# Pair sums of the gate and up products: diagonal results copied by ScalarE, banks opened with differences

## The chip, the cores and the metric

One Trainium2 chip, one of its cores. The metric is device time in microseconds. All data are float32. The engines are named as the profile names them: PE (TensorE, matmul), PEld (its weight loads), DVE (VectorE), ACT (ScalarE), POOL (GpSimd) and SP (SyncE, which issues most DMAs).

## The reference: what is computed

A residual layer of gated experts on x of shape (8, 512, 256), with 8 experts and one shared expert of width F = 1024:

```
g = einsum('bsd,edf->ebsf', h, Wg);  u = einsum('bsd,edf->ebsf', h, Wu)
expert_outs = einsum('ebsf,efd->ebsd', silu(g) * u, Wd)
expert_output = einsum('be,ebsd->bsd', gating_probs, expert_outs)
shared = einsum('bsf,fd->bsd', silu(h @ Sg) * (h @ Su), Sd)
x = x + (1 - sg) * expert_output + sg * shared
```

The kernel treats the shared expert as a ninth one. What follows is about g and u: for every expert, block of 128 columns of F and batch, a 128x512 result with a contraction over 256.

## The kernel before, in words

The work is cut into 36 *units*: 2 halves of four batches, 9 experts, 2 groups of four 128-column blocks (lines 249 to 261). A unit needs, for m = 0 (gate) and m = 1 (up), all 16 products c_ij of weight block i and batch j. A product has two halves of the contraction and would be two matmuls. The kernel saves matmuls: with numbers CI = (0, 1, -1, 2) given to the four blocks, it shifts batch i's first half by CI (line 163) and block i's second half by CI (`make_at`, line 286), so that a *diagonal* product is exact:

- `P_step` (line 370): P_i is the first matmul of c_ii. ACT copies it out of PSUM to SBUF (line 377).
- `Q_step` (line 402): the second matmul lands on the same bank (line 404), which then holds c_ii = P_i + Q_i. DVE takes Q_i = c_ii - P_i out of it (line 410).
- The two off-diagonal products of a pair (i, j), six pairs in `PAIRS`, cost three matmuls in place of four. `R1_step` (line 424) multiplies the difference of weights U by the difference of batches V (line 432), called UV below. Then c_ij = (P_i + Q_j) - UV + W_0 B_0 and c_ji = (P_j + Q_i) + UV + W_1 B_1; `R_step` (line 439) does the last matmul of each (line 445).

The sums z_ij = P_i + Q_j, and where they are made, are what the change is about. For most pairs POOL makes them from SBUF copies (line 389); for `ZBANK` = 2 pairs one of the two sums is made by DVE from the bank that still holds P (line 391). DVE then writes z_ij - UV into a fresh bank (line 436) and adds z_ji onto the bank of UV (line 437). For two *late* pairs (`LATE`, or `LATE0` in the first unit) no z is made: P alone goes in at lines 436 and 437, and DVE adds Q after the last matmul (line 450). In the first unit pair 0 is `PLAIN`: four matmuls for two products, for each m (line 417), and no forms of x before them; its forms are made later for the other units (`make_forms`, line 171).

`finish` (line 355) ends a product: for m = 0 ACT takes silu of the bank (line 358), for m = 1 DVE multiplies silu, gate weight and bank (line 364) into h. `down` (line 467) multiplies h with the down weights with two PSUM banks of its own, `po`, which ACT opens with the running sum (line 482) and copies back (line 506).

Order: PE and POOL keep the order of the program text, ACT does so in the first unit, and a scheduler places DVE, the rest of ACT and SP when the kernel is built. PE's order is written in strings (lines 621 to 624): G is one step of gate and up, D one matmul of the down product of the unit before. Within a unit the G steps are: Q0, P1, P2, Q1, Q2, P3, R1 of pair 0, Q3 (two each, m = 0 and 1), then for each pair p and each m: R1 of pair p + 1, and two R of pair p. The first unit has no D. Gate and up have three PSUM banks for each m (`ps_g`), so a new bank waits for a `finish`.

Of the kernel before, what the change touches and what calls it, by code (L numbers as in the profile page):

```python
# [9 lines left out]
F32 = mybir.dt.float32  # L10
AF = mybir.ActivationFunctionType
ALU = mybir.AluOpType
# [4 lines left out]
def kernel(  # L17
# [31 lines left out]
    nc = tc.nc  # L49
    B, S, D = x.shape  # L50
    E, _, F = Wg.shape
    P = 128
# [4 lines left out]
    NH = B // NI  # L57
    CI = (0.0, 1.0, -1.0, 2.0)
    PAIRS = ((1, 0), (0, 2), (3, 0), (1, 2), (3, 1), (3, 2))
    ZBANK = 2  # L60
    LATE = (4, 5)
    LATE0 = (3, 5)

    PLAIN = (0,)

    const = ctx.enter_context(tc.tile_pool(name="const", bufs=1))
    wpool = ctx.enter_context(tc.tile_pool(name="w", bufs=5))
# [5 lines left out]
    ppool = ctx.enter_context(tc.tile_pool(name="p", bufs=16))  # L73
# [4 lines left out]
    zpool = ctx.enter_context(tc.tile_pool(name="z", bufs=6))  # L78
# [7 lines left out]
    ps_o = ctx.enter_context(tc.tile_pool(name="ps_o", bufs=1, space=PSUM))  # L86
# [4 lines left out]
    gp = nc.gpsimd  # L91
    ve = nc.vector
# [31 lines left out]
    turned = [False, False]  # L124
# [60 lines left out]
    def store_made():  # L185
        for h, p, tiles in made:
            scratch[h, p] = dram.tile([P, 3, S], F32, tag=f"xs{h}_{p}", name=f"xs{h}_{p}")
            for k, t in enumerate(tiles):
                nc.sync.dma_start(scratch[h, p][:, k], t)
        made.clear()  # L190
# [59 lines left out]
    for h in range(NH):  # L250
        for e in range(NE):
            for g in range(GRP):
                u = Unit()
                u.n, u.h, u.e, u.g = len(units), h, e, g
                u.opens = e == 0 and g == 0
                u.closes = e == NE - 1 and g == GRP - 1
                u.name = f"{h}_{e}_{g}"
                u.raw, u.at, u.U, u.W, u.V, u.VB = {}, {}, {}, {}, {}, {}
                u.Ps, u.Qs, u.z, u.bank, u.h_ = {}, {}, {}, {}, {}
                u.wd, u.T, u.sg, u.store = {}, {}, {}, []  # L260
                units.append(u)

# [23 lines left out]
    def make_at(u, i):  # L286
# [9 lines left out]
            return  # L296
        scaled_sum(t, CI[i], raw[:, :, 0], raw[:, :, 1], False)
        u.at[i] = t

    def late(u):  # L300
        return LATE if u.n else LATE0

    def plain(u, p):
        return u.n == 0 and p in PLAIN

# [43 lines left out]
                1: a11, 2: a12, 3: s[:, 3], 4: a22, 5: s[:, 0], 6: s[:, 1], 7: s[:, 2]  # L349
            }  # L350

    def new_bank(u, m, name):
        return ps_g.tile([P, S], F32, tag=f"g{m}", name=f"{name}{m}_{u.name}")

    def finish(u, m, i, j, bank):
        if m == 0:
            s = spool.tile([P, S], F32, tag="sg", name=f"sg{i}{j}_{u.name}")
            nc.scalar.activation(s, bank, AF.Silu)  # L358
            u.sg[i, j] = s
        else:  # L360
            b = NI * u.h + j
            pool, tag = (hapool, "ha") if j < 2 else (hbpool, "hb")
            t = pool.tile([P, S], F32, tag=tag, name=f"h{i}{j}_{u.name}")
            ve.scalar_tensor_tensor(  # L364
                t, u.sg[i, j], coef[:, u.e, b : b + 1], bank, ALU.mult, ALU.mult
            )
            u.h_[i, j] = t


    def P_step(u, i, m):  # L370
        bank = new_bank(u, m, f"c{i}{i}")
        u.bank[i, i, m] = bank
        nc.tensor.matmul(  # L373
            bank, u.raw[i][:, m, 0], xhub[u.h, i][:, 0], start=True, stop=True
        )
        t = ppool.tile([P, S], F32, tag="p", name=f"P{i}{m}_{u.name}")
        nc.scalar.copy(t, bank)  # L377
        u.Ps[i, m] = t
        for p in range(ZBANK):
            a, b = PAIRS[p]  # L380
            if max(a, b) == i and not plain(u, p):
                new_z(u, p, m, i, bank if u.n or p else None)

    def new_z(u, p, m, i, bank=None):

        o = sum(PAIRS[p]) - i
        z = zpool.tile([P, S], F32, tag="z", name=f"z{i}{o}{m}_{u.name}")
        if bank is None:
            gp.tensor_tensor(z, u.Ps[i, m], u.Qs[o, m], ALU.add)  # L389
        else:  # L390
            ve.tensor_add(z, bank, u.Qs[o, m])  # L391
        u.z[i, o, m] = z

    def make_z(u, p, m):
        if p in late(u) or plain(u, p):
            return
        for i in PAIRS[p]:
            o = sum(PAIRS[p]) - i
            if (i, o, m) not in u.z:
                new_z(u, p, m, i)  # L400

    def Q_step(u, i, m):
        bank = u.bank[i, i, m]
        nc.tensor.matmul(  # L404
            bank, u.at[i][:, m], xhub[u.h, i][:, 1],
            start=False, stop=True, skip_group_check=True,
        )
        finish(u, m, i, i, bank)
        t = ppool.tile([P, S], F32, tag="p", name=f"Q{i}{m}_{u.name}")
        ve.tensor_sub(t, bank, u.Ps[i, m])  # L410
        u.Qs[i, m] = t

    def plain_step(u, p, m, r, k):
        i, j = PAIRS[p] if r == 0 else PAIRS[p][::-1]
# [6 lines left out]
        if k:  # L421
            finish(u, m, i, j, u.bank[i, j, m])

    def R1_step(u, p, m):
        i, j = PAIRS[p]
        if plain(u, p):
            for k in range(2):
                plain_step(u, p, m, 0, k)
            return
        bank = new_bank(u, m, f"c{j}{i}")  # L430
        u.bank[j, i, m] = bank
        nc.tensor.matmul(bank, u.U[p][:, m], u.V[p], start=True, stop=True)  # L432
        seed = new_bank(u, m, f"c{i}{j}")
        u.bank[i, j, m] = seed
        first = u.Ps if p in late(u) else u.z
        ve.tensor_sub(seed, first[(i, m) if p in late(u) else (i, j, m)], bank)  # L436
        ve.tensor_add(bank, bank, first[(j, m) if p in late(u) else (j, i, m)])  # L437

    def R_step(u, p, m, r):
        if plain(u, p):  # L440
            plain_step(u, p, m, 1, r)
            return
        i, j = PAIRS[p] if r == 0 else PAIRS[p][::-1]
        bank = u.bank[i, j, m]
        nc.tensor.matmul(  # L445
            bank, u.W[p][:, r, m], u.VB[p][:, r],
            start=False, stop=True, skip_group_check=True,
        )
        if p in late(u):
            ve.tensor_add(bank, bank, u.Qs[j, m])  # L450
        finish(u, m, i, j, bank)


# [98 lines left out]
    def gate_up(u, nxt):  # L552

        def differences(p):
            x_difference(u, p)
            w_difference(u, p)

        def sums(p):
            x_sums(u, p)
            w_sums(u, p)  # L560

        for p, make in ((0, w_difference), (0, w_sums), (1, w_difference), (1, w_sums)):
            make(u, p)
        if u.n:
            make_at(u, 3)
        w_difference(u, 2)
        ahead = ((0, x_difference), (0, x_sums), (1, x_difference), (1, x_sums), (2, x_difference))
        if u.n:
            for p, make in ahead:
                make(u, p)  # L570
        for kind, i in (
            ("Q", 0), ("P", 1), ("P", 2), ("Q", 1), ("Q", 2), ("P", 3), ("R", 0), ("Q", 3),
        ):
            for m in range(2):
                if kind == "Q":
                    Q_step(u, i, m)
                    if i == 1:
                        make_z(u, 0, m)
                    if i == 3:
                        make_z(u, 1, m)  # L580
                elif kind == "P":
                    P_step(u, i, m)
                    if u.n == 0 and m == 1 and i in (1, 3):
                        for p, make in ahead[:2] if i == 1 else ahead[2:]:
                            make(u, p)
                else:
                    R1_step(u, 0, m)
                yield
        for p in range(len(PAIRS)):
            last = p + 1 == len(PAIRS)  # L590
            if p + 3 < len(PAIRS):
                differences(p + 3)
            if nxt is not None:
                if p >= 2:
                    load_w(nxt, p - 2)
                    if p < 5:
                        make_at(nxt, p - 2)
            store_forms(u)
            if u.n == 0 and p == 4:
                for q in PLAIN:  # L600
                    make_forms(0, q)
            if p == 5:
                store_made()
            for m in range(2):
                if not last:
                    R1_step(u, p + 1, m)
                elif nxt is not None:
                    P_step(nxt, 0, m)
                yield
                if p + 2 < len(PAIRS):  # L610
                    make_z(u, p + 2, m)
                for r in range(2):
                    R_step(u, p, m, r)
                    if p == 5 and m == 0 and r == 1:
                        T_sums(u, 0, 5)
                        load_d(u, (0,))
                    if m == 1 and r == 1 and p + 2 < len(PAIRS):
                        sums(p + 2)
                    yield
# [129 lines left out]
```

## Time and profile before

| what | value |
|---|---|
| time, median of 3 runs | 2517.44 us (2516.77 to 2517.63) |
| the profiled execution's own time | 2517.02 us |
| its span in the trace | 2514.9 us |
| busy in the span: PE | 2498.6 us, 99% |
| POOL | 1922.3 us, 76% |
| DVE | 1492.6 us, 59% |
| ACT | 1143.4 us, 45% |
| PE's busy time from 0 to 80 us, in steps of 20 | 17.86, 19.30, 15.98, 20.00 us |
| DVE's busy time in the same steps | 8.54, 15.55, 19.15, 17.09 us |
| DMA | mean 97 GB/s |

A 128x512 float32 matmul is two records in the trace, so 5900 PE records are some 2,950 matmuls and transposes. Busy time is the length of all records of an engine without overlap; the mean duration that a group shows (592 ns for a 128x512 matmul) is that of one record, and records overlap. From one matmul to the next in a full stream it is 0.858 us. Idle time of an engine that is not the bound costs nothing by itself; what counts is PE's idle time, 16 us of the span, and whether new work ends before PE needs it.

### The profile page before, as it was taken

Reading aid. Unit: us, or ns where it says so; the run is one execution under the profiler, and the core shown is the slowest. Engines: PE = TensorE matmul, PEld = TensorE weight load, DVE = VectorE, ACT = ScalarE, POOL = GpSimd, SP = SyncE. Lnnn points to the kernel's source line nnn. Section 1 sums busy time; section 2 is a strip of 40 time slices with the busy share of each in tenths; the row PEclk is TensorE's granted clock in tenths of the full one; section 3 lists DMA queues with packets and bytes.
Section 4 is the critical chain, followed back from the end, with each engine's and each line's share of the span. In section 5 each row is a group of like instructions: output and inputs, shape, how many; then the busy total and the mean of one; then the engine's idle time right before and its main releaser. Section 6 shows DMA issues by size and latency. Waiting matters only on the chain.

```text
span 2514.9 us, 22103 instructions
## 1 busy us (share of the span) xinstructions
PE 2498.6 (99%) x5900; PEld 1108.3 (44%) x5900; DVE 1492.6 (59%) x2242; ACT 1143.4 (45%) x2078; POOL 1922.3 (76%) x2080
## 2 busy tenths in 40 slices
PE   8999999999999999999999999999999999999999
PEld 3444444444444444444444444444444444444444
DVE  7655555565555555565785555555555555555556
ACT  3344444444444444444333444444444444444443
POOL 6877877777777778877798777877777777777874
PEclk9999999999999999999999999999999999999999
DMA  4332232233333323233444322323233332332222
GB/s 159 116 90 84 88 95 89 84 101 96 100 92 93 92 88 88 85 93 94 151 135 119 98 88 84 92 88 89 88 95 100 97 96 88 100 88 81 89 85 80
DMA packets 181180, 242.94 MB, mean 97 GB/s; under 512 B 13888, under 2 KB 122432, under 8 KB 181056
## 3 DMA queue, kind: packets, MB, share of 16 engines
q1 hardware_dynamic: 180768, 241.49, 32.0%
q8 instruction: 49, 0.80, 0.1%
q14 instruction: 75, 0.61, 0.1%
q10 hardware_dynamic: 288, 0.04, 0.0%
HBM read 227.84 MB, written 13.63 MB: 96 GB/s over the span
## 4 chain that ended last, share of the span: by engine, by line
PE 97%; DVE 1%; issue 0%; DMA 0%; POOL 0%; ACT 0%; SPq 0%; DVEq 0%; ACTq 0%
PE po L491 34%; PE c L445 29%; PE c L432 14%; PE c L373 10%; PE c L404 10%; DMA xin<-in_x_dram 0%; PE pto L136 0%; PE ptx L136 0%; POOL z L389 0%; DVE h L364 0%; DVE v L200 0%; PE c L417 0%; DVE c L436 0%; DVE c L437 0%; DVE b L216 0%
## 5 line engine op out<-in xcount | busy, mean ns | idle before, releaser
L445 PE MATMUL c<-b,wb 128*128 128x512 f32 x1720 | 810.6, 592 | 1.0 <-DVE c L436 0.5
L389 POOL TENSOR_TENSOR z<-P,Q 128x512 f32<-128x512 f32 x430 | 538.4, 1281 | 111.0 <-DVE Q L410 69.0
L364 DVE SCALAR_TENSOR_TENSOR h<-sg,coef,c 128x512 f32<-128x512 f32 x576 | 427.1, 742 | 231.6 <-PE c L445 221.6
L506 ACT COPY acc<-po 128x512 f32<-128x512 f32 x477 | 279.0, 585 | 589.0 <-PE po L491 586.1
L358 ACT ACTIVATE sg<-c 128x512 f32<-128x512 f32 x576 | 342.4, 595 | 382.2 <-PE c L445 196.0
L445 PEld LDWEIGHTS c<-b,wb 128*128 128x128 f32 x1720 | 325.9, 190 | 409.6 <-issue 387.3
L464 POOL TENSOR_TENSOR T<-h,h 128x512 f32<-128x512 f32 x284 | 358.3, 1278 | 137.1 <-PE po L491 92.8
L491 PE MATMUL po<-T,sd 128*128 128x512 f32 x864 | 435.3, 593 | 2.0 <-ACT to L543 1.6
L432 PE MATMUL c<-v,u 128*128 128x512 f32 x860 | 433.7, 592 | 3.0 <-DVE h L364 2.0
L436 DVE TENSOR_TENSOR c<-z,c 128x512 f32<-128x512 f32 x286 | 198.6, 694 | 330.2 <-ACT sg L358 255.7
L464 POOL TENSOR_TENSOR T<-h,T 128x512 f32<-128x512 f32 x284 | 356.5, 1278 | 6.8 <-PE po L491 6.8
L450 DVE TENSOR_TENSOR c<-c,Q 128x512 f32<-128x512 f32 x288 | 200.4, 697 | 187.2 <-PE c L445 186.9
L284 POOL TENSOR_TENSOR wb<-wb,u 128x256 f32<-128x256 f32 x216 | 154.5, 738 | 204.6 <-ACT wb L283 204.6
L491 PE MATMUL po<-h,wd 128*128 128x512 f32 x576 | 293.5, 592 | 0.0
L482 ACT COPY po<-acc 128x512 f32<-128x512 f32 x465 | 274.3, 590 | 32.9 <-DVE acc L508 16.9
L373 PE MATMUL c<-x,w 128*128 128x512 f32 x576 | 277.1, 594 | 0.0
L410 DVE TENSOR_TENSOR Q<-c,P 128x512 f32<-128x512 f32 x288 | 198.0, 688 | 106.5 <-ACT sg L358 106.4
L432 PEld LDWEIGHTS c<-v,u 128*128 128x128 f32 x860 | 163.2, 190 | 209.7 <-issue 187.0
L491 PEld LDWEIGHTS po<-T,sd 128*128 128x128 f32 x864 | 163.3, 190 | 206.6 <-issue 187.1
L377 ACT COPY P<-c 128x512 f32<-128x512 f32 x288 | 168.0, 584 | 130.9 <-PE c L373 130.9
L404 PE MATMUL c<-x,at 128*128 128x512 f32 x432 | 203.3, 592 | 0.7 <-DVE z L391 0.7
L437 DVE TENSOR_TENSOR c<-c,z 128x512 f32<-128x512 f32 x286 | 198.1, 693 | 0.0
(73 smaller groups left out, 1882.0 us busy)
## 6 DMA issues: line engine op xcount, KB each, us to landing
b<-xs SPq DMA_DIRECT2D x207, 512.0 KB, 3.6
v<-xs SPq DMA_DIRECT2D x207, 256.0 KB, 2.6
w<-in_L_cond_Wg_dram SPq DMA_DIRECT2D x128, 128.0 KB, 3.3
w<-in_L_cond_Wu_dram SPq DMA_DIRECT2D x128, 128.0 KB, 3.3
wd<-in_L_cond_Wd_dram SPq DMA_DIRECT2D x64, 256.0 KB, 2.7
xin<-in_x_dram SPq DMA_DIRECT2D x16, 256.0 KB, 4.1
xs<-b SPq DMA_DIRECT2D x8, 512.0 KB, 3.1
xr<-in_x_dram SPq DMA_DIRECT2D x16, 256.0 KB, 3.2
```

What stands on the lines that cost most here:

```text
L358: nc.scalar.activation(s, bank, AF.Silu)
L364: ve.scalar_tensor_tensor(t, u.sg[i, j], coef[:, u.e, b : b + 1], bank, ALU.mult, ALU.mult)
L373: nc.tensor.matmul(bank, u.raw[i][:, m, 0], xhub[u.h, i][:, 0], start=True, stop=True)
L389: gp.tensor_tensor(z, u.Ps[i, m], u.Qs[o, m], ALU.add)
L404: nc.tensor.matmul(bank, u.at[i][:, m], xhub[u.h, i][:, 1], start=False, stop=True, skip_group_check=True,)
L432: nc.tensor.matmul(bank, u.U[p][:, m], u.V[p], start=True, stop=True)
L445: nc.tensor.matmul(bank, u.W[p][:, r, m], u.VB[p][:, r], start=False, stop=True, skip_group_check=True,)
L450: ve.tensor_add(bank, bank, u.Qs[j, m])
L464: eng.tensor_tensor(t, a, b, ALU.subtract)
L482: nc.scalar.copy(po, acc[J, x])
L491: nc.tensor.matmul(po, u.wd[I][x], b, start=first, stop=True, skip_group_check=not first,)
L506: nc.scalar.copy(acc[J, x], po)
```

## The change

Q is no longer made. ACT copies the finished diagonal result D_i = P_i + Q_i out of PSUM instead. For pair (i, j) the kernel makes one difference f = P_j - P_i, in place of two sums. The bank of c_ji is opened with f by an ACT copy (`seed`, called ahead of the step), UV is accumulated on it, and DVE makes the bank of c_ij as D_j minus that bank, since D_j - (P_j - P_i) - UV = P_i + Q_j - UV. After the last matmul of c_ji DVE adds D_i. All pairs are handled alike: there are no late and no plain pairs. The differences of pairs 0 to 2 are made by DVE while P is in its bank, those of pairs 3 to 5 by POOL. In the first unit some banks are taken from `ps_o`.

```diff
-    ZBANK = 2
-    LATE = (4, 5)
-    LATE0 = (3, 5)
-
-    PLAIN = (0,)
+    FBANK = 3
+
+    PLAIN = ()
...
-    def new_bank(u, m, name):
+    def new_bank(u, m, name, spare=False):
+
+        if spare and u.n == 0:
+            turned[m] = False
+            return ps_o.tile([P, S], F32, tag=f"po{m}", name=f"{name}{m}_{u.name}")
         return ps_g.tile([P, S], F32, tag=f"g{m}", name=f"{name}{m}_{u.name}")
...
     def P_step(u, i, m):
-        bank = new_bank(u, m, f"c{i}{i}")
+        bank = new_bank(u, m, f"c{i}{i}", i == 3)
...
-        for p in range(ZBANK):
-            a, b = PAIRS[p]
-            if max(a, b) == i and not plain(u, p):
-                new_z(u, p, m, i, bank if u.n or p else None)
+        for p in range(FBANK):
+            if max(PAIRS[p]) == i:
+                make_f(u, p, m, bank)
+
+    def make_f(u, p, m, bank=None):
+
+        if plain(u, p) or (p, m) in u.f:
+            return
+        i, j = PAIRS[p]
+        f = zpool.tile([P, S], F32, tag="z", name=f"f{i}{j}{m}_{u.name}")
         if bank is None:
-            gp.tensor_tensor(z, u.Ps[i, m], u.Qs[o, m], ALU.add)
+            gp.tensor_tensor(f, u.Ps[j, m], u.Ps[i, m], ALU.subtract)
+        elif i > j:
+            ve.tensor_sub(f, u.Ps[j, m], bank)
         else:
-            ve.tensor_add(z, bank, u.Qs[o, m])
+            ve.tensor_sub(f, bank, u.Ps[i, m])
+        u.f[p, m] = f
...
         finish(u, m, i, i, bank)
-        t = ppool.tile([P, S], F32, tag="p", name=f"Q{i}{m}_{u.name}")
-        ve.tensor_sub(t, bank, u.Ps[i, m])
-        u.Qs[i, m] = t
+        t = ppool.tile([P, S], F32, tag="p", name=f"D{i}{m}_{u.name}")
+        nc.scalar.copy(t, bank)
+        u.Ds[i, m] = t
...
+    def seed(u, p):
+
+        i, j = PAIRS[p]
+        for m in range(2 if not plain(u, p) else 0):
+            u.bank[j, i, m] = new_bank(u, m, f"c{j}{i}", p % 2 == 1)
+            nc.scalar.copy(u.bank[j, i, m], u.f[p, m])
+
     def R1_step(u, p, m):
...
-        bank = new_bank(u, m, f"c{j}{i}")
-        u.bank[j, i, m] = bank
-        nc.tensor.matmul(bank, u.U[p][:, m], u.V[p], start=True, stop=True)
-        seed = new_bank(u, m, f"c{i}{j}")
-        u.bank[i, j, m] = seed
-        first = u.Ps if p in late(u) else u.z
-        ve.tensor_sub(seed, first[(i, m) if p in late(u) else (i, j, m)], bank)
-        ve.tensor_add(bank, bank, first[(j, m) if p in late(u) else (j, i, m)])
+        bank = u.bank[j, i, m]
+        nc.tensor.matmul(
+            bank, u.U[p][:, m], u.V[p], start=False, stop=True, skip_group_check=True
+        )
+        other = new_bank(u, m, f"c{i}{j}")
+        u.bank[i, j, m] = other
+        ve.tensor_sub(other, u.Ds[j, m], bank)
...
-        if p in late(u):
-            ve.tensor_add(bank, bank, u.Qs[j, m])
+        if r == 1:
+            ve.tensor_add(bank, bank, u.Ds[j, m])
         finish(u, m, i, j, bank)
...
+            if kind == "P" and i == 3:
+                seed(u, 0)
             for m in range(2):
                 if kind == "Q":
                     Q_step(u, i, m)
-                    if i == 1:
-                        make_z(u, 0, m)
-                    if i == 3:
-                        make_z(u, 1, m)
...
+            if not last:
+                seed(u, p + 1)
             for m in range(2):
                 if not last:
                     R1_step(u, p + 1, m)
...
                 if p + 2 < len(PAIRS):
-                    make_z(u, p + 2, m)
+                    make_f(u, p + 2, m)
```

More of the change, by code (lines that the diff above doesn't have):

```diff
@@ L258 @@
                 u.raw, u.at, u.U, u.W, u.V, u.VB = {}, {}, {}, {}, {}, {}
-                u.Ps, u.Qs, u.z, u.bank, u.h_ = {}, {}, {}, {}, {}
+                u.Ps, u.Ds, u.f, u.bank, u.h_ = {}, {}, {}, {}, {}
                 u.wd, u.T, u.sg, u.store = {}, {}, {}, []
@@ L298, in make_at @@
         u.at[i] = t
-    def late(u):
-        return LATE if u.n else LATE0
     def plain(u, p):
@@ L378, in P_step @@
         u.Ps[i, m] = t
-        for p in range(ZBANK):
-            a, b = PAIRS[p]
-            if max(a, b) == i and not plain(u, p):
-                new_z(u, p, m, i, bank if u.n or p else None)
-    def new_z(u, p, m, i, bank=None):
-        o = sum(PAIRS[p]) - i
-        z = zpool.tile([P, S], F32, tag="z", name=f"z{i}{o}{m}_{u.name}")
+        for p in range(FBANK):
[6 more added lines that the diff above has]
+        f = zpool.tile([P, S], F32, tag="z", name=f"f{i}{j}{m}_{u.name}")
         if bank is None:
-            gp.tensor_tensor(z, u.Ps[i, m], u.Qs[o, m], ALU.add)
-        else:
[L391 to L400, printed above, removed]
+            gp.tensor_tensor(f, u.Ps[j, m], u.Ps[i, m], ALU.subtract)
+        elif i > j:
+            ve.tensor_sub(f, u.Ps[j, m], bank)
+        else:
+            ve.tensor_sub(f, bank, u.Ps[i, m])
+        u.f[p, m] = f
     def Q_step(u, i, m):
```

## The prediction, made before the changed kernel ran

> **What bounds the kernel now.** I read the page's busy times and chain first, then PE's own timeline, then one unit in the middle.
>
> ```profile
> span 2514.9 us, 22103 instructions
> PE 2498.6 (99%) x5900; PEld 1108.3 (44%) x5900; DVE 1492.6 (59%) x2242; ACT 1143.4 (45%) x2078; POOL 1922.3 (76%) x2080
> PE 97%; DVE 1%; issue 0%; DMA 0%; POOL 0%; ACT 0%; SPq 0%; DVEq 0%; ACTq 0%
> ```
>
> The chain that ends last runs 97% through PE. PE idles 16.3 us of the span. PE's timeline puts 5.2 us of that in the last 75 us, 4.2 us between 1190 and 1345 us (where the second half's x is turned), and nothing in the other long stretches: from 130 to 1190 us it is busy 1060.00 of 1060 us, from 1345 to 2440 us 1095.00 of 1095. The rest is in the first unit; some of its lines (start, length, instruction, idle time before and what ended it):
>
> ```profile
> 20.31 1.10 PE L404 MATMUL c<-x,at 128*128 128x512 f32 x2 [0.20 <-DVE z L391]
> 21.90 1.12 PE L404 MATMUL c<-x,at 128*128 128x512 f32 x2 [0.49 <-DVE z L391]
> ...
> 29.73 1.02 PE L432 MATMUL c<-v,u 128*128 128x512 f32 x2
> ...
> 44.70 1.13 PE L432 MATMUL c<-v,u 128*128 128x512 f32 x2 [0.92 <-DVE h L364]
> ...
> 53.74 1.10 PE L432 MATMUL c<-v,u 128*128 128x512 f32 x2 [1.05 <-ACT sg L358]
> ...
> 58.36 1.12 PE L432 MATMUL c<-v,u 128*128 128x512 f32 x2 [1.05 <-DVE h L364]
> ```
>
> By start times against 0.858 us a matmul, PE loses 6.8 us from 18.22 to 61.04 us (42.82 us for 42 matmuls). So in 34 units the change can only cost; in the first it can win some.
>
> **What the skill says.** *Perfetto Trace Analysis*, "Identifying the Most-Contended Engine": matmul busy share is a bad measure, since pipelined matmuls hide gaps. I therefore use start times: in the full stretches they are 0.858 us apart without exception, and the two measures agree. *PSUM — Partial Sum Buffer*, "PSUM bank collisions raise a hardware error": two engines must not touch a bank at once, readers included. The trace agrees: DVE's Q waits for ACT's silu of the same bank, 106 us in all. So the new copy D (ACT) of an m = 1 bank queues behind DVE's h of it. *SBUF — State Buffer*, on the pair of ports that DVE and GpSimd share: a DVE operation with two SBUF inputs is blocked by GpSimd's. The trace agrees: v and b at lines 200 and 216 take 1.02 to 1.42 us in places, against 0.69 us with a PSUM input.
>
> **The change, part by part.** Instructions in each of 36 units, with durations from these rows:
>
> ```profile
> L389 POOL TENSOR_TENSOR z<-P,Q 128x512 f32<-128x512 f32 x430 | 538.4, 1281 | 111.0 <-DVE Q L410 69.0
> L482 ACT COPY po<-acc 128x512 f32<-128x512 f32 x465 | 274.3, 590 | 32.9 <-DVE acc L508 16.9
> L410 DVE TENSOR_TENSOR Q<-c,P 128x512 f32<-128x512 f32 x288 | 198.0, 688 | 106.5 <-ACT sg L358 106.4
> L377 ACT COPY P<-c 128x512 f32<-128x512 f32 x288 | 168.0, 584 | 130.9 <-PE c L373 130.9
> ```
>
> - POOL: 12 sums become 6: 6 x 1.28 x 36 = 277 us less (76% to 65%).
> - DVE: loses 8 Q, 4 z, 12 of the 24 bank sums and 8 late adds, gains 6 f and 12 adds of D: 14 fewer x 0.69 x 36 = 348 us less (59% to 45%).
> - ACT: gains 8 copies D (0.584, the row of P) and 12 openings (0.590, the row of po): 20 x 0.587 x 36 = 423 us more (45% to 62%).
> - PE: two fewer matmuls, since pair 0 of the first unit takes 6, not 8: -1.7 us, inside the first unit's sum. PE's order is otherwise the same.
> - SP: the first unit stores pair 0's forms early in two DMAs, not late in three. The next readers are in the second unit; at 97 GB/s mean this is hidden.
>
> In 34 units none of that is on PE's path unless a new wait is late. The new waits: R1 needs ACT's opening, which needs f and a free bank; line 437 needs D; c_ji is finished after one more DVE add. I laid the built order of ACT, DVE and POOL over PE's measured starts in the unit that begins at 613.8 us and looked for each opening how long before its R1 it ends: pair 0 8 us or more (m = 0), pair 2 1.1, pair 3 1.0 (it waits for POOL's f at 34.3 us of the unit), pair 4 1.9, pair 5 0.9. The tight one is pair 1 (m = 0). Its bank is that of c_33, free only after silu and D:
>
> ```profile
> 630.98 1.88 PE L404 MATMUL c<-x,at 128*128 128x512 f32 x4
> 631.18 0.58 ACT L506 COPY acc<-po 128x512 f32<-128x512 f32 x1 [2.23 <-PE po L491]
> 631.79 0.59 ACT L482 COPY po<-acc 128x512 f32<-128x512 f32 x1
> 632.32 0.59 ACT L358 ACTIVATE sg<-c 128x512 f32<-128x512 f32 x1
> ...
> 634.41 1.02 PE L432 MATMUL c<-v,u 128*128 128x512 f32 x2
> ```
>
> The two copies for the down product stay ahead of silu in the built order, so silu starts at 632.32 again. An independent ACT instruction starts 0.49 us after the one before (1234.26 and 1234.75, two copies), a dependent one 0.62 us (631.18 to 631.79). D: 632.81. Opening: 633.43, ends 633.43 + 0.59 = 634.02. PE wants it at 634.41; after a wait PE restarts some 0.15 us late (21.16 + 0.68 = 21.84, then 21.90 with 0.10 us more than an unstalled pair). So 0.24 us are left. Where ACT's D could be bounded: from the 0.49 us spacing (0.24 us left) to full serial execution of silu, D and opening, 0.62 each (about 0.1 left). I take no stall, cost 0; each 0.1 us that the chain is over would cost 34 x 0.1 = 3.4 us.
>
> First unit. ACT's order is that of the text, so an ACT instruction that waits holds all behind it. By the same method:
> - D01 waits for h00, which DVE does after v and b of pair 0 (forms that the plain pair did without; 0.7 to 1.1 us each). x2's copy, then P1, stand behind D01: PE's P2 starts at 17.25, not 16.50.
> - Openings of pair 0 stand behind D1 and D2: R1 of pair 0 at 25.4 where PE is ready at 24.1. Then Q3 waits 0.75 us for f.
> - Opening of pair 1 stands behind silu, D30, D31 (which waits for DVE's v and h33) and the scaling of v: ends 32.2, R1 at 32.35 where the kernel before has 29.73: 2.6 us behind.
> - Openings of pairs 2, 3 and 5 stand behind ACT's wb, which waits until the last R frees a wb buffer: 1.6, 2.05 and 1.55 us, 5.2 us in all.
> - Both kernels have 30 matmuls left there, 25.75 us, up to the next unit's P; the kernel before, which starts that at 61.04, loses 5.6 us among them. So PE reaches it at 32.35 + 25.75 + 5.2 = 63.3: **+2.3 us**. Bounds: -2 if D01 and v3 don't hold ACT as long, +5 if each wait is half a microsecond longer.
>
> The stretch from 1190 to 1345 us: there a scaling of v (0.62 us) and po and turn copies are ahead of the tight opening; its silu moves from 1256.49 to 1257.4, so R1 due at 1258.59 waits some 0.75 us. Three waits for the turn copy (0.73, 0.73, 0.85 us in the trace) can each grow by one ACT instruction, half on average: 0.8 us. **+1.6 us**, bounds 0 to +4.
>
> The tail keeps its chain (down products, DVE's acc): 0. Sum against the profiled execution's own time: 2517.0 + 2.3 + 1.6 = 2520.9; the median of the runs is 0.4 above that execution, so **2521.3 us**.
>
> **Rivals.** A change of 0.2%, 5.0 us, is about what a measurement of this kernel can tell from none.
> - *B, slower: the tight opening is late in every unit.* One mechanism: ACT's silu, D33 and opening before R1 of pair 1. For it: no slack elsewhere is below 0.9 us, this one is 0.24, and ACT sits 62% busy in order. Against: the durations are all measured. It decides from 0.24 us on; at twice that slack of extra delay (0.5 us) the cost is 0.26 x 34 = 8.8 us: 2530 us. Worse cases (another bank than I think, so a whole 0.6 us instruction more) give 2541.
> - *C, faster: the first unit was DVE's.* DVE is busy 19.15 of the 20 us from 40 to 60 us and loses some of its operations there. If ACT doesn't take its place, the 6.8 us of stalls and 1.7 us of matmuls go: 2517.4 - 8.5 = 2509 us. Against: ACT's fixed order above.
> - *D: nothing at all*, both ends outside PE's path: 2517 us; it lies within A's range.
>
> **How the numbers follow.** A, my forecast, with D: 0.65, range 2515 to 2526 by the two bounds; a third of it is over 2522.5. B 0.25, C 0.10. Faster by over 0.2% (under 2512.4): C's most, 0.08. Slower (over 2522.5): B and A's third, 0.25 + 0.22 = 0.47. Within: 0.45. For 8 in 10 the range reaches into both: 2512 to 2531.
>
> **What would show it.** ACT's busy time near 1566 us, DVE's 1145, POOL's 1645. Right: PE busy 1060 of 1060 us in the middle stretch, and the new stalls of PE named "ACT c" at line 432 before 62 us, with P of the second unit near 63.3 us. Wrong by B: a stall before line 432 once in each unit, released by ACT's opening. Wrong by C: P of the second unit before 58 us.

## The result, and the profile after

The changed kernel takes 2521.94 us (median of 14 runs, 2519.69 to 2526.16), the kernel before on the same chip 2516.61 us (14 runs, 2514.41 to 2517.66): a ratio of 1.0023, 95% interval 1.0015 to 1.0032. The forecast was 2521.3 us in a range of 2512 to 2531. The profiled execution took 2520.21 us, 3.19 us more than that of before.

From the page of the changed kernel: span, busy times, shares of the chain that ended last.

```profile
span 2518.4 us, 21862 instructions
...
PE 2497.1 (99%) x5896; PEld 1107.9 (44%) x5896; DVE 1213.0 (48%) x1744; ACT 1493.3 (59%) x2798; POOL 1662.4 (66%) x1868
...
PE 98%; DMA 1%; DVE 0%; ACT 0%; issue 0%; SPq 0%; DVEq 0%; ACTq 0%
```

POOL and DVE are relieved by 260 and 280 us, ACT is loaded by 350, and nothing of that reaches the time: the chain is PE, as before. Where PE stood still is read by stretch (start and end, length, PE busy and its records, granted clock, DMA share, GB/s):

```profile
12.00:62.00 50.00, 40.90 (x100) 0.97 0.42 151
...
130.00:1190.00 1060.00, 1060.00 (x2473) 1.00 0.31 91
1190.00:1345.00 155.00, 150.54 (x391) 1.00 0.41 134
1345.00:2440.00 1095.00, 1095.00 (x2555) 1.00 0.31 93
```

The two long stretches are full, so 34 units cost nothing. From 12 to 62 us PE is busy 40.90 us (before: 45.28), and it is the only stretch here whose granted clock is below 1.00. PE's waits (what waited, for whom: us in total, times, longest):

```profile
PE c L432 <- ACT c L423: 8.2, 5, 2.6
PE ptx L134 <- DMA xin<-in_x_dram: 3.0, 4, 1.1
PE po L491 <- ACT to L543: 2.3, 3, 0.8
...
PE c L398 <- DVE f L391: 0.5, 1, 0.5
```

"ACT c" at line 432 is R1 waiting for an opening by `seed`; all five are in the first unit. PE's timeline shows them one by one (start, length, instruction, idle time before and what ended it):

```profile
24.59 1.96 PE L432 MATMUL c<-v,u 128*128 128x512 f32 x4 [1.14 <-ACT c L423]
27.06 1.99 PE L398 MATMUL c<-x,at 128*128 128x512 f32 x4 [0.52 <-DVE f L391]
31.68 1.10 PE L432 MATMUL c<-v,u 128*128 128x512 f32 x2 [2.64 <-ACT c L423]
32.62 3.29 PE L445 MATMUL c<-b,wb 128*128 128x512 f32 x4
35.69 1.36 PE L432 MATMUL c<-v,u 128*128 128x512 f32 x2
...
40.06 1.13 PE L432 MATMUL c<-v,u 128*128 128x512 f32 x2 [1.29 <-ACT c L423]
...
47.29 1.12 PE L432 MATMUL c<-v,u 128*128 128x512 f32 x2 [1.82 <-ACT c L423]
...
59.16 1.13 PE L432 MATMUL c<-v,u 128*128 128x512 f32 x2 [1.30 <-ACT c L423]
...
64.41 1.02 PE L372 MATMUL c<-x,w 128*128 128x512 f32 x2
```

The last line is P of the second unit, at 64.41 us; before it stands at 61.04 us, so 3.37 of the span's 3.5 us are lost by here. One thing in these lines is no wait: the four records that start at 32.62 take 3.07 us to the next start instead of 1.72. The clock by microsecond (same columns as the stretches):

```profile
32.00:33.00 1.00, 1.00 (x3) 0.97 0.58 223
33.00:34.00 1.00, 1.00 (x3) 0.50 0.06 16
34.00:35.00 1.00, 1.00 (x3) 0.50 0.00 0
35.00:36.00 1.00, 1.00 (x3) 0.50 0.00 0
36.00:37.00 1.00, 1.00 (x3) 0.82 0.00 0
```

After the longest wait, PE ran at half its clock for 3.4 us, which costs 1.7 us.

The tight opening in the middle, in the unit of the prediction. ACT's timeline, then PE's:

```profile
634.54 0.58 ACT L506 COPY acc<-po 128x512 f32<-128x512 f32 x1 [2.23 <-PE po L491]
635.16 0.59 ACT L482 COPY po<-acc 128x512 f32<-128x512 f32 x1
635.69 0.59 ACT L357 ACTIVATE sg<-c 128x512 f32<-128x512 f32 x1
636.17 0.58 ACT L404 COPY D<-c 128x512 f32<-128x512 f32 x1
636.78 0.59 ACT L423 COPY c<-f 128x512 f32<-128x512 f32 x1
```

```profile
637.78 1.02 PE L432 MATMUL c<-v,u 128*128 128x512 f32 x2
```

The opening ends at 637.37, 0.41 us before R1 starts; less the 0.15 us that PE needs to restart, 0.26 us are left (prediction: 0.24).

### The profile page after: what moved, and what is told of

Same layout as the page of the kernel before. It is cut to its first block, busy times and chain, and to the rows that moved or that the text cites. A ratio compares the mean times of both kernels' runs of the same rounds, so it can differ in the third digit from the quotient of the medians.

```text
span 2518.4 us, 21862 instructions
## 1 busy us (share of the span) xinstructions
PE 2497.1 (99%) x5896; PEld 1107.9 (44%) x5896; DVE 1213.0 (48%) x1744; ACT 1493.3 (59%) x2798; POOL 1662.4 (66%) x1868
## 4 chain that ended last, share of the span: by engine, by line
PE 98%; DMA 1%; DVE 0%; ACT 0%; issue 0%; SPq 0%; DVEq 0%; ACTq 0%
PE po L491 34%; PE c L445 29%; PE c L432 15%; PE c L398 10%; PE c L372 10%; DMA xin<-in_x_dram 1%; PE ptx L134 0%; PE pto L134 0%; DVE h L363 0%; ACT c L423 0%; DVE acc L508 0%; ACT to L543 0%; ACT wb L281 0%; DVE x L160 0%; DVE acc L512 0%
## 5 line engine op out<-in xcount | busy, mean ns | idle before, releaser
L437 DVE TENSOR_TENSOR c<-D,c 128x512 f32<-128x512 f32 x432 | 299.7, 694 | 307.9 <-ACT sg L357 283.4
L450 DVE TENSOR_TENSOR c<-c,D 128x512 f32<-128x512 f32 x432 | 300.2, 695 | 213.4 <-PE c L445 212.8
L423 ACT COPY c<-f 128x512 f32<-128x512 f32 x432 | 255.7, 592 | 150.1 <-DVE h L363 114.7
L389 POOL TENSOR_TENSOR f<-P,P 128x512 f32<-128x512 f32 x216 | 272.6, 1277 | 0.0
L404 ACT COPY D<-c 128x512 f32<-128x512 f32 x288 | 168.0, 583 | 51.4 <-DVE h L363 51.3
```

Of the source, the lines that this page charges most:

```text
L437: ve.tensor_sub(other, u.Ds[j, m], bank)
L450: ve.tensor_add(bank, bank, u.Ds[j, m])
```

## The experiments

All are edits of the changed kernel. Each set of runs shares runs of the kernel before on its chip, and kernels of different sets are compared by their distance from it (changed kernel: 5.3 us). "P3 to P" is the time on PE's timeline from the start of the first unit's P3 to the second unit's P; it leaves out the first 20 us, in which profiles differ by up to 2.2 us with no edit there (P3 at 21.33 us in slack_512, at 23.50 in seed1_early). The first unit before has 38 matmuls in that stretch, the changed one 36, which alone is 1.72 us. "Clock" is the mean granted clock of the runs. It covers the whole span, so also the last microseconds, where PE has no work left and a lower clock costs nothing: in the profile of f_early PE's last instruction starts at 2505.00 us, the first half-clock stretch comes after 2507 us, and the mean is 0.999 all the same. What a clock is worth in microseconds is therefore an estimate below.

| kernel | median us (runs) | before, same chip | ratio, 95% interval | P3 to P, us | clock |
|---|---|---|---|---|---|
| before | | | | 38.18 | 0.9996 |
| changed | 2521.94 (14) | 2516.61 | 1.0023, 1.0015 to 1.0032 | 42.85 | 0.9988 |
| seed1_early | 2520.94 (21) | 2516.41 | 1.0015, 1.0009 to 1.0022 | 39.10 | 0.9988 |
| seed_before_wb | 2524.11 (7) | 2516.41 | 1.0031, 1.0020 to 1.0042 | 43.13 | 0.9980 |
| both_seeds | 2518.58 (13) | 2516.41 | 1.0004, 0.9996 to 1.0012 | 36.49 | 0.9989 |
| old_first | 2519.05 (21) | 2516.41 | 1.0008, 1.0002 to 1.0015 | 38.18 | 0.9989 |
| forms_later | 2521.81 (13) | 2515.51 | 1.0023, 1.0014 to 1.0031 | 42.85 | 0.9987 |
| f_early | 2515.16 (13) | 2515.51 | 0.9998, 0.9989 to 1.0006 | 34.91 | 0.9992 |
| all_moves | 2513.33 (21) | 2515.51 | 0.9989, 0.9983 to 0.9996 | 35.18 | 0.9993 |
| slack_512 | 2545.49 (4) | 2515.51 | 1.0119, 1.0105 to 1.0134 | | 0.9985 |
| slack_256 | 2526.07 (5) | 2516.38 | 1.0042, 1.0030 to 1.0055 | | 0.9986 |
| store_pool | 2527.48 (5) | 2516.38 | 1.0043, 1.0030 to 1.0057 | | 0.9976 |
| f_early_store_pool | 2518.54 (21) | 2516.38 | 1.0012, 1.0005 to 1.0018 | | 0.9980 |
| old_first_store_pool | 2522.04 (14) | 2516.38 | 1.0022, 1.0014 to 1.0030 | | 0.9981 |

**seed1_early.** The longest wait taken away by order alone.

```diff
-            u.bank[j, i, m] = new_bank(u, m, f"c{j}{i}", p % 2 == 1)
+            u.bank[j, i, m] = new_bank(u, m, f"c{j}{i}", p in (2, 4))
...
+            if kind == "Q" and i == 3 and u.n == 0:
+                seed(u, 1)
...
-            if not last:
+            if not last and not (u.n == 0 and p == 0):
                 seed(u, p + 1)
```

> In the first unit alone, pair 1's two openings are issued ahead of Q3, into the bank that c_22 leaves; pairs 2 and 4 take the spare banks. Theory 1 (the stall before pair 1's R1 is ACT's order: the opening stands behind silu, D30, D31 and the scaling of v, and the half clock after it follows from the length of the idle time): the 2.64 us wait goes, and with it the stretch from 32.6 to 36.9 us at half clock, 1.7 us. PE's P of the second unit at about 60.1 us instead of 64.41, time about 2517.6. Theory 2 (the wait is the data's: f, or the bank, is late whatever the order): the wait stays within 0.5 us, time about 2521.5. Theory 3 (the half clock comes at this time whatever PE does): the wait goes, the 1.7 us stay, about 2519.3.

```profile
28.85 1.98 PE L398 MATMUL c<-x,at 128*128 128x512 f32 x4 [0.52 <-DVE f L391]
30.67 1.02 PE L432 MATMUL c<-v,u 128*128 128x512 f32 x2
...
37.28 1.12 PE L432 MATMUL c<-v,u 128*128 128x512 f32 x2 [1.30 <-ACT c L423]
```

R1 of pair 1 (30.67) follows Q3 without a wait, and the granted clock is 1.00 from 20 to 62 us. P3 to P falls by 3.75 us, of which a new wait of 0.71 us before pair 4 took its part. So theory 1 holds for the wait and for the half clock, and theory 3 falls: the half clock came from the idle time. The time that theory 1 expected, 2517.6 us, was missed: the median is 2520.94, still 4.5 us above the kernel before. What the profile shows of that: half-clock stretches elsewhere, from about 7.6 to 11 us and around 1221 us, and 3.5 us of waits for x at the turn of the halves, 1.6 more than in the changed kernel.

**seed_before_wb.** The other three waits, by order.

```diff
                     if m == 1 and r == 1 and p + 2 < len(PAIRS):
+                        if u.n == 0:
+                            seed(u, p + 2)
                         sums(p + 2)
...
-            if not last:
+            if not last and not (u.n == 0 and p > 0):
                 seed(u, p + 1)
```

> In the first unit alone, the openings of pairs 2 to 5 are issued ahead of ACT's scaling of wb and of v. Theory 1 (the openings are late because they stand behind wb, which waits for a buffer): the waits of 1.29, 1.82 and 1.30 us go, the one of 2.64 us and the half clock stay; P of the second unit at about 60.0 us, time about 2517.5. Theory 2 (the bank or POOL's f is late by itself, so that the order of ACT matters little): at least half of the 4.4 us stay, time 2519.7 or more, and the waits move to f or to the last finish of the bank's product.

```profile
44.63 1.12 PE L432 MATMUL c<-v,u 128*128 128x512 f32 x2 [0.77 <-ACT c L423]
...
48.80 1.12 PE L432 MATMUL c<-v,u 128*128 128x512 f32 x2 [1.32 <-ACT c L423]
...
53.23 1.12 PE L432 MATMUL c<-v,u 128*128 128x512 f32 x2 [1.59 <-ACT c L423]
...
59.41 1.13 PE L432 MATMUL c<-v,u 128*128 128x512 f32 x2 [0.76 <-DVE c L450]
```

Theory 2: 4.44 us of waits where there had been 4.41. ACT's timeline names the next ones late: an opening at 43.99 waits for POOL's f, one at 48.16 for DVE's h, which frees the bank, those at 52.59 and 54.26 for POOL's f. ACT's order was one of several things that were late by about the same. The median lies 2.4 us further above the kernel before than that of the changed kernel, though P3 to P is only 0.28 us longer; the profile has a half-clock stretch of 3.4 us at the turn (from about 1220.3 us) that the changed kernel's has not.

**both_seeds.** Both edits, with the condition `u.n == 0` on the old place.

> Both moves of openings together, first unit alone. If the two are separate waits in series, their gains add: 8.7 us, P of the second unit at about 55.7 us, time about 2513.2, which would be below the kernel before by 3.4 us. If another engine stands just behind ACT (DVE, by the rival forecast of the first unit), the sum is less: 2515 to 2517.

P3 to P is 6.36 us shorter than in the changed kernel, and shorter than before by the 1.7 us of its two matmuls. The gains don't add to 8.7: waits of 0.66 and 1.23 us for openings behind POOL's f stay (pairs 3 and 4), and one of 0.78 us before R1 of pair 5. That one is put down to DVE's add (line 450), which ends at 54.49 us, but the opening, which also waited for POOL's f, ends only 0.02 us before it. The median, 2518.58 us, is above both expectations.

**f_early.** As both_seeds, and POOL makes f of pairs 3 to 5 in its idle time.

```diff
+            if kind == "R" and u.n == 0:
+                for m in range(2):
+                    make_f(u, 3, m)
...
                 seed(u, 1)
+                for m in range(2):
+                    make_f(u, 4, m)
...
                             seed(u, p + 2)
+                            if p == 0:
+                                for k in range(2):
+                                    make_f(u, 5, k)
```

> Both moves of openings in the first unit, and POOL makes the differences f of pairs 3, 4 and 5 there before the b and wb of pair 2, in time in which it stood idle (11.65 us in the changed kernel). Theory 1 (with ACT's order mended, the openings of pairs 3 to 5 wait for POOL's f): the waits of 0.66 and 1.23 us before R1 go, from both_seeds 1.9 us less: P of the second unit 34.6 us after the start of P3 (both_seeds 36.5), median about 2516.7. Theory 2 (DVE, which reads with two SBUF inputs beside POOL, is next and keeps PE where it was): less than 0.7 us is won, 2518.

```profile
39.99 1.10 PE L432 MATMUL c<-v,u 128*128 128x512 f32 x2 [0.78 <-ACT c L423]
...
46.26 1.10 PE L432 MATMUL c<-v,u 128*128 128x512 f32 x2 [0.88 <-ACT c L423]
...
56.63 1.02 PE L372 MATMUL c<-x,w 128*128 128x512 f32 x2
```

P3 to P is 34.91 us, 1.58 less than in both_seeds and 0.3 short of what theory 1 expected. But the gain is not where theory 1 put it. No opening waits for POOL's f any more, yet the waits before R1 of pairs 3 and 4 are still 0.78 and 0.88 us (both_seeds: 0.66 and 1.23). ACT's timeline shows what is late there now, silu and the scaling of v, which wait for DVE:

```profile
38.76 0.60 ACT L357 ACTIVATE sg<-c 128x512 f32<-128x512 f32 x1 [2.35 <-DVE c L450]
39.25 0.59 ACT L423 COPY c<-f 128x512 f32<-128x512 f32 x1
...
43.69 0.63 ACT L200 ACTIVATE v<-v 128x512 f32<-128x512 f32 x1 [2.39 <-DVE v L198]
```

The wait before R1 of pair 5 is gone, and 1.08 of the 1.58 us are won behind pair 4. So POOL's f was late in all three places, and in two of them DVE stood right behind it, which is the mechanism of theory 2. The time equals that of the kernel before.

In seed1_early, both_seeds and f_early the median gains 0.8, 3.2 and 5.7 us on the changed kernel, where P3 to P gains 3.75, 6.36 and 7.94. Where the other 2 to 3 us go is not shown.

**old_first.** The first unit as before, the other 35 as changed.

```diff
     def P_step(u, i, m):
+        if u.n == 0:
+            old_P_step(u, i, m)
+            return
```

The same for `Q_step`, `R1_step` and `R_step`; the `old_` functions, `make_z` and the plain pair are those of the kernel before.

> The first unit in the form of the kernel before (sums z, Q, late pairs, a plain pair), the other 35 in the changed form. If all the loss lies in the first unit: P of the second unit at 61.0 us, time 2516.6 to 2517.3 (0.7 us of waits for x at the turn of the halves may stay). If the 35 units cost something that the one profiled execution does not show: 2519 or more.

P3 to P is 38.18 us, that of before to the last digit, and the long stretches are full. But 2519.05 us is at the edge of "something in the 35 units". The mean granted clock goes with it: 0.9989 against 0.9996 is 0.0007 x 2519 = 1.8 of the 2.6 us (an estimate). The six runs with a mean clock of 1.000 have a median of 2516.39 us, that of the kernel before; the fifteen others have 2520.21. So nothing is lost in the runs that keep their clock. Why the others lose it is not shown. In the profile, half-clock stretches lie at 8 to 11 us and, right after PE's two waits for x at the turn of the halves (1.50 and 0.27 us), at about 1216.2 to 1219.6 us.

**forms_later.** Why x is late at the turn. SP's queue in the kernel before, then in the changed one (xs<-f is the store of the forms, xin the load of the last batch):

```profile
1204.32 4.36 SPq L189 DMA_DIRECT2D xs<-f  x3
...
1209.26 0.87 SPq L142 DMA_DIRECT2D xin<-in_x_dram  x2
```

```profile
1207.17 6.81 SPq L187 DMA_DIRECT2D xs<-f  x3
...
1214.56 0.87 SPq L140 DMA_DIRECT2D xin<-in_x_dram  x2
```

SP stands at the store 2.45 us longer, and the load comes 5.30 us later where the unit runs 3.36 us later. The store waits for POOL's part of a form, which starts at 1212.36 us, before at 1207.07: two of POOL's differences f (1206.55 and 1211.14 us) now stand close ahead of it. The edit makes each form three G steps later, which puts the load first:

```diff
-                    if nG in (33, 39, 45):
-                        make_forms(u.h + 1, (nG - 33) // 6)
-                    if nG in (39, 45, 51):
+                    if nG in (36, 42, 48):
+                        make_forms(u.h + 1, (nG - 36) // 6)
+                    if nG in (42, 48, 51):
```

> At the turn of the halves alone: the forms of the next half's first three pairs are made one turn step later, so that on SP's queue the load of the last batch of x stands ahead of the store of the forms, which held SP for 6.8 us in the changed kernel. Theory 1 (PE's waits for x there, 1.07 and 0.86 us, come from SP standing at that store): both go, the load is issued right after the transposes of the batch before, PE busy from 1190 to 1345 us rises by 1.9 us in span, time about 2520.0 instead of 2521.9; less if a half-clock stretch after the idle goes with it (another 1.7 us in the executions that have one). Theory 2 (the transfer itself is slow there because the weights share the DMA engines): the waits stay within 0.5 us, time 2521.5 to 2522.

```profile
1224.91 2.08 PE L491 MATMUL po<-h,sd 128*128 128x512 f32 x2 [2.74 <-DVE x L160]
```

The load is issued at 1212.52, in front of the store, and both waits for x are gone: SP was their cause. But DVE, which now makes the forms between the last batches, frees the po bank late, and PE waits 2.74 us for that, with half the clock until about 1231 us. The wait was replaced, and nothing is won: 6.3 us above the kernel before.

**all_moves.** f_early and forms_later together.

> The moves of openings and of f in the first unit, and the forms one step later at the turn of the halves. If the three places are in series: f_early less 1.6 us of waits for x, about 2515, or 2514 if half-clock stretches become fewer too; below the kernel before (2516.4). If the turn has another wait just behind: 2516 to 2517, no difference from the kernel before.

2513.33 us: faster than the kernel before by 0.11% (0.04 to 0.17), too little for the 0.2% that the prediction set as its bound. That the turn is mended is not shown: PE is busy 151.14 us there, f_early 151.07, with 1.60 us of wait for DVE in place of 1.40 for x. What makes its median 1.8 us lower than that of f_early I could not find in the two profiles, and their intervals overlap.

**slack_512 and slack_256.** The slack of the tight opening, measured by eating it up: a second copy of the same values.

```diff
         nc.scalar.copy(t, bank)
+        if u.n and i == 3 and m == 0:
+            nc.scalar.copy(t[:, 0:512], bank[:, 0:512])
         u.Ds[i, m] = t
```

> In every unit but the first, ACT copies D of c_33 (m = 0) a second time, 128x512, ahead of the tight opening; in the built order D of c_33 (m = 1) then also comes ahead of it. So the opening is two copies later: 2 x 0.49 = 0.98 us against a slack of 0.26 us. If the slack is what decides (the price that the rival forecast B put on it): a stall of about 0.7 us before R1 of pair 1 in each of some 34 units, 24 us, time about 2546. If D of m = 1 has to wait for DVE's h33 on top, up to 1.3 us each and 2566. If the opening has other cover than the slack: within 3 us of 2521.9.

> As slack_512, but the repeated copy of D is 128x256, and in the built order nothing else slips ahead of the opening. By 0.18 us less for 256 columns (590 and 408 ns, rows of po and wb) it adds about 0.30 us to the chain, against a slack of 0.26 us. If the slack is what decides: 0 to 0.1 us a unit, 2522 to 2525. If ACT's opening ends where PE can't see it because of other cover: 2521.9. If the slack is smaller than read (0.1 us): 0.2 us a unit, 2528.7.

slack_512, PE's waits and the first long stretch (two lines are added, so 434 and 425 are 432 and 423):

```profile
PE c L434 <- ACT c L425: 23.8, 38, 2.6
```

```profile
130.00:1190.00 1060.00, 1053.06 (x2446) 1.00 0.31 91
```

33 waits more than in the changed kernel. In one unit silu to opening takes 640.77 to 642.83, 2.06 us where the changed kernel has 1.09: 0.97 us are added, and PE loses 0.73: x 34 = 24.8 us (measured: 30.0 above the kernel before, less 5.3, is 24.7). slack_256, ACT and PE in the unit of the prediction:

```profile
636.73 0.59 ACT L357 ACTIVATE sg<-c 128x512 f32<-128x512 f32 x1
637.22 0.58 ACT L404 COPY D<-c 128x512 f32<-128x512 f32 x1
637.82 0.37 ACT L406 COPY D<-c 128x256 f32<-128x256 f32 x1
638.23 0.59 ACT L425 COPY c<-f 128x512 f32<-128x512 f32 x1
```

```profile
638.87 1.13 PE L434 MATMUL c<-v,u 128*128 128x512 f32 x2
```

Silu to opening is 1.50 us, 0.41 added. Unstalled, R1 would start at 638.82; it starts 0.05 us late and takes 0.10 us longer. That is too short to be listed as a wait, and 0.15 x 34 = 5.1 us for the kernel (measured: 9.7 less 5.3, 4.4). Both give the slack as added less lost: 0.97 - 0.73 = 0.24 and 0.41 - 0.15 = 0.26 us.

**store_pool, f_early_store_pool, old_first_store_pool.** The store moved off SP another way, on the changed kernel, f_early and old_first.

```diff
-                nc.sync.dma_start(scratch[h, p][:, k], t)
+                gp.dma_start(scratch[h, p][:, k], t)
```

> At the turn of the halves alone: the forms of the next half's first pairs are made where the changed kernel makes them, but POOL's queue issues their store, so that SP can load the last batch of x. Theory 1 (SP's stand of 6.8 us at the store makes x late; the wait that came in its place when the forms were made later was that lateness of DVE's work): PE's two waits for x (1.93 us) go and no other takes their place, time about 2520.0, or 2518.5 if half-clock stretches after the idle go too. Theory 2 (PE's idle at the turn is kept by a chain of transposes and copies that is too long for its place, whatever SP does): another wait of 1.5 us or more, time 2521.5 or more.

> The mended first unit (openings ahead, f early) and the store on POOL's queue. If the first unit and the turn are separate: f_early (2515.2) less 1.5 us, 2513.6, about as all_moves (2513.3) or a little below. If the turn's idle stays: 2515.

> The first unit in the old form, the other 35 in the new one, the store on POOL's queue. If what old_first lost against the kernel before (2519.05 against 2516.4) comes from the turn of the halves: 2516.4 or below. If it has another place: within 1 us of 2519.

All three are 2.5 to 5.8 us slower than without the edit. The waits for x go, as theory 1 said, and a larger one comes. In store_pool, DVE and then PE:

```profile
1229.62 6.02 DVE L176 TENSOR_TENSOR f<-x,x 128x512 f32<-128x512 f32 x1 [1.73 <-DMA xs<-f]
...
1239.78 0.75 DVE L363 SCALAR_TENSOR_TENSOR h<-sg,coef,c 128x512 f32<-128x512 f32 x1
```

```profile
1240.58 2.08 PE L372 MATMUL c<-x,w 128*128 128x512 f32 x2 [5.43 <-DVE h L363]
```

POOL issues the stores at 1225.91 us, behind a form that it reaches late; the next form of DVE reuses a stored tile, so it waits for the store, and then its row is 6.02 us long (why so long is not shown). The h of 1239.78 us, which frees the bank that PE's P needs, stands behind it, behind another h and behind the form's second operation (2.20 us at 1236.34). What old_first loses at the turn is therefore not settled by its run.

## Why the prediction was right, point by point

- **The middle: no stall.** Right; both long stretches are full. The 0.24 us of slack are 0.24 to 0.26 by the two slack runs and 0.26 by the trace.
- **The first unit, stall by stall.** Right in place and size. R1 of pair 0 was to wait 1.3 us and waited 1.31 (24.59 less 21.56 + 1.72); Q3 0.75 and 0.75 (27.06 less 24.59 + 1.72). The three openings behind wb were to cost 1.6 + 2.05 + 1.55 = 5.2 us; start to start they cost 1.45 + 1.97 + 1.46 = 4.88, and 0.1 us each for the slower first matmul: 5.18. seed1_early shows that ACT's order made the longest. For those behind wb the order was the last to be late, but not alone: seed_before_wb shows h and f right behind it.
- **The sum of the first unit, +2.3 us.** It was 3.37. Missing is the halved clock, 1.7 us. It is made up in part by a start that was 0.7 us earlier at R1 of pair 1 (31.68, not 32.35): the first P of the profile of before took 2.58 us where 1.72 are due, which I took as the kernel's own.
- **The turn, +1.6 us.** The step failed. The waits for the turn copy are 0.68, 0.73 and 0.85 us and did not grow, and the scaling of v did not hold the opening: in that unit it starts at 1261.96 and ends at 1262.55, R1 starts at 1262.75. Silu is only 0.22 us later against PE than before (1260.87 and 1262.75; 1256.49 and 1258.59), not 0.9; and by the prediction's own spacings 0.9 would have cost 0.66 us, not 0.75. From the second unit to 1290 us the lag grows by 0.66 us, at places that the prediction did not name: 0.38 at four transposes (1207.23 us) that wait for DVE's form and for x in turn, 0.41 at the two waits for x behind SP's store; 0.13 is won back. "This is hidden" on SP was said of the first unit's stores; the later stores, whose forms come later now, were not looked at.
- **The tail, 0.** The lag falls from 4.02 us at 1340 to 3.63 at 2497: a wait of 0.15 us (0.4 start to start) in the last unit of before is gone, which I had not foreseen.
- **Median above profile, +0.4 us.** It was 1.7. By the clock column the changed kernel loses 0.0012 x 2520 = 3.0 us a run to a reduced clock and the kernel before 1.0, about 2 of the 5.3 us between the medians. This is an estimate: it takes the part after PE's last instruction to be the same in both, which is not shown. The rest would be the stalls.
- **Busy times.** Forecast 1566, 1145 and 1645 us for ACT, DVE and POOL, measured 1493, 1213 and 1662. The term was mis-sized: I multiplied by the length of a row, but busy time counts overlap once. ACT gained 350 us in 720 copies, 0.486 each, which is the spacing of two independent ones, not their 0.587; DVE lost 280 us in 498 instructions, 0.56 each, not 0.69.
- **Rival B** is not what happened, but its mechanism and its price are right once the chain is made longer: 24.7 us for 0.97 us added.
- **Rival C** failed for the reason given, ACT's fixed order. With the order alone mended (both_seeds) the first unit is 1.7 us shorter than before from P3 on, which is its two matmuls; with POOL's f early as well (f_early) it is 3.3 us shorter. So a part of that gain was there to have.

So the mechanism was right in the middle and in the first unit, and wrong at the turn. That the total came within 0.6 us is in part luck: I took 0.9 us too much at the turn, 0.7 at R1 of pair 1 and 0.4 in the tail, and left out what the clock takes, 1.7 us in the first unit of the profile and more in the median.

Not settled: why every kernel with the new form in 35 units shows a lower mean clock than before, old_first too. Half-clock stretches were seen at four places: the start, the first unit, the turn and the end. Only that of the first unit was taken away at will. That of the end stands in all 14 profiles, begins 1.5 to 5 us after PE's last instruction, lasts from 0.2 to 3.2 us and costs nothing; a part of the differences in the mean clock may be no more than this.

## What to carry to other kernels

When work is moved to an engine with time to spare, look for its order before its load: ACT at 59% cost nothing in 34 units and several us in the one in which an instruction that waits holds the openings behind it. Take a wait away only after asking what is second; here most of the places had something else late by about the same (the bank, f, DVE's add, DVE's form), and three of the five moves (the openings ahead of wb, the later forms, the store on POOL) by themselves only put another wait in its place. Measure a slack by eating it up: a copy of known length gave 0.24 to 0.26 us in a kernel whose runs lie up to 6.5 us apart.

## What the runs showed of the hardware

The Trainium skill, *TensorE: Matmul & The Clock Gate*, "What's actually happening", says that the PE clock is halved after an idle window of about 3.4 us, that the window runs freely, and that it takes as long again to come back. The half rate and the 3.4 us agree (0.50 from about 33.0 to 36.4 us). The length of idle time does not: all six profiles with the wait of 2.6 us before R1 of pair 1 have a half-clock stretch between 20 and 40 us, all eight others have a clock of 1.00 there. Waits of 1.8 us in the changed kernel had none behind them; at the turn, where transposes lie between two waits, 1.50 + 0.27 us had (old_first), while 1.77 + 0.90 us had not (slack_512), so that the sum of such waits doesn't decide it. Longer waits had one, of 3.4 us or of about twice that: 6.8 us after 2.74 us of waiting in forms_later, 3.4 us after 5.43 us in store_pool. So a stall of 2.6 us before R1 of pair 1 costs another 1.7 us here, more than half its own length.

In the kernel before, the record says 1.00 from 7 to 11 us, while two matmuls took 2.58 us there instead of 1.72: start times showed a slowness that the clock line does not. Whether it was the clock is not shown.
